# Softmax sums of a transformer block: from pairs of key tiles to running sums over four

## The chip, the cores and the metric

The kernel runs on one core of a Trainium2 chip. The metric is the device time in microseconds (us) of one execution. The engines of the core work side by side, each through its own queue in order: TensorE (PE; its weight loads are shown as PEld), VectorE (DVE), ScalarE (ACT), GpSimd (POOL), and SyncE (SP), which here only issues DMAs. An instruction waits at the head of its queue until what it needs is there, and everything behind it in that queue waits with it.

## What is computed

One pre-norm transformer block in float32 on `x` of 2 x 1024 x 1024, with 32 heads of 32 columns:

```python
qkv = layernorm(x) @ attn_qkvw + attn_qkvb            # 1024 -> 3 x 1024
scores = einsum('bhqd,bhkd->bhqk', q, k) / sqrt(32)
probs = softmax(scores, axis=-1)
x = x + (probs @ v) @ attn_ow + attn_ob
h = layernorm(x)
x = x + (silu(h @ W_gate.T) * (h @ W_up.T)) @ W_down.T  # 1024 -> 2752 -> 1024
```

The softmax needs, for each query, the sum of its 1024 exponentials. The change concerns how this sum is formed.

## The kernel before

**Blocks and units.** Attention is cut into four blocks, here 0 to 3: two batches times two halves of 512 queries (`self.phase` in the code is the block). A block has 16 units, and a unit is two heads by 512 queries. A unit's keys are eight key tiles of 128, so a key tile `p` is a float32 tile of 128 keys by 1024 (two heads by 512 queries). Beside block 0 TensorE runs the projections to Q, K and V; beside blocks 1 to 3 it runs the output projection and the feed-forward of the block before (a seven-product scheme for the matrices, lines 908 to 1090). After block 3 the last feed-forward runs alone.

**What happens to a key tile.** In this order:

1. TensorE makes the scores into PSUM (L509). VectorE takes a running maximum over the tiles (`top`, L525), ScalarE copies the scores to SBUF (`p`, L528).
2. After all eight tiles, VectorE reduces `top` to one negative maximum per query (L548 to L567), which goes through DRAM and comes back on all partitions as `m` (`m<-d`, L575).
3. `less_maximum` adds `m` to the tile: on GpSimd, in block 0 every fourth time on VectorE (L582). ScalarE takes the exponential in place (L591).
4. `add` adds exponentials of neighbouring tiles into each other (L605).
5. `values` has TensorE multiply the tile by the unit's values (`acc<-p,vals`) and, for those tiles in which a sum is complete (`summed`), by a tile of ones (`acc<-p,ones`), both at L620. One such product of a tile is a set of four matmuls that fill four column ranges of the array at once. The ones products give the softmax sums.

**Sums before the change.** In blocks 1 to 3 sums are over two tiles: tile 1 becomes p0+p1, tile 3 becomes p2+p3, and so on. So tiles 1, 3, 5 and 7 get a ones product. Additions for tiles 1 and 5 are GpSimd's, those for 3 and 7 VectorE's. In block 0 sums are over four tiles as a tree, all on VectorE: p1 += p0, p3 += p2, then p3 += p1; so only tiles 3 and 7 get a ones product. As tiles are overwritten with sums, their values have to be replaced by differences, so that the products still add up to the sum of p times v. `differences` (L593) does this on GpSimd once per unit: one operation over 256 columns (L596), and a second one over 128 in block 0 (L599).

**Order.** The kernel sets the order of all instructions itself. `attention_steps` (L650) makes a list of paced steps, called beats, one for each key tile, and the `Emitter` (L44) weaves them into a list of other TensorE work, so that they stand at even distances by planned costs (855 ns for four matmuls' worth). Work of other engines is put off with `em.later(delay, ...)`: it is written down once the planned clock has gone on by so many ns. A tile's subtraction is written at beat n, its exponential 3500 ns later, an addition 8100 ns after the subtraction of the same tile (the third one of block 0: 9900 ns). Value products are written for four tiles together (`RUN`), three beats after the subtraction of the last of the four, once its addition is written. These delays set only the order in the queues; semaphores set the time.

Two things bound this: PSUM has three tiles (`lps`, tag `lin`) for the results of projections and feed-forward, which VectorE and ScalarE read out (for instance L938 to L951 and L1086), and tiles `p` come from a ring of 19 (`RING`).

Of the kernel before, what the change touches and what calls it, by code (L numbers as in the profile page):

```python
# [12 lines left out]
ALU = mybir.AluOpType  # L13
# [117 lines left out]
def preln_block_kernel(  # L131
# [14 lines left out]
    nc = tc.nc  # L146
# [16 lines left out]
    LAG = 3  # L163
    RUN = 4
    RING = NT + LAG + RUN + 4

    const = ctx.enter_context(tc.tile_pool(name="const", bufs=1))
    lin = ctx.enter_context(tc.tile_pool(name="lin", bufs=1))
# [25 lines left out]
    def Pt(name):  # L194
        return att.tile([P, S], F32, tag="p", bufs=RING, name=name)

# [32 lines left out]
    em = Emitter()  # L229
# [234 lines left out]
    class Unit:  # L464
# [114 lines left out]
        def less_maximum(self, kt):  # L579
            p = self.p[kt]  # L580
            eng = nc.vector if self.phase == 0 and kt % 4 == 3 else nc.gpsimd
            eng.tensor_tensor(p, p, self.m, ALU.add)  # L582
            em.later(3500.0, lambda: self.exponential(kt))
            if kt % 2 == 1:
                twice = self.phase == 0 and kt % 4 == 3
                em.later(8100.0, lambda: self.add(kt, 1), None if twice else ("added", self.n, kt))
                if twice:
                    em.later(9900.0, lambda: self.add(kt, 2), ("added", self.n, kt))

        def exponential(self, kt):  # L590
            nc.scalar.activation(self.p[kt], self.p[kt], AF.Exp, scale=SCALE)  # L591

        def differences(self):  # L593

            v = self.v.rearrange("p (i a) n -> p i a n", a=2)
            nc.gpsimd.tensor_tensor(v[:, :, 0, :], v[:, :, 0, :], v[:, :, 1, :], ALU.subtract)  # L596
            if self.phase == 0:
                v = self.v.rearrange("p (i a) n -> p i a n", a=4)
                nc.gpsimd.tensor_tensor(v[:, :, 1, :], v[:, :, 1, :], v[:, :, 3, :], ALU.subtract)  # L599

        def add(self, kt, back):


            eng = nc.vector if self.phase == 0 or kt % RUN == RUN - 1 else nc.gpsimd
            eng.tensor_tensor(self.p[kt], self.p[kt], self.p[kt - back], ALU.add)  # L605

        def summed(self, kt):
            return kt % (4 if self.phase == 0 else 2) == (3 if self.phase == 0 else 1)

        def values(self, kt):  # L610

# [536 lines left out]
    def weight_sum_steps():  # L1148
        q = Steps()

        def start(i):
# [42 lines left out]
            for j, args in enumerate(todo):  # L1194
                em.later(8500.0 + 3000.0 * j, lambda args=args: add(*args))
                em.later(16000.0 + 2500.0 * j, lambda j=j: store(j))
# [158 lines left out]
```

## Time and profile before

| | us |
|---|---|
| median of 3 runs | 3277.49 |
| lowest and highest of them | 3269.68, 3278.75 |
| the profiled execution | 3264.24 |
| its span, first to last instruction | 3262.5 |

Busy time by engine and the stages of the span are in rows shown further below. Some groups of instructions that matter here, with how often they ran, the busy time in all and the mean of one:

| line, engine | what | count | busy us | mean ns |
|---|---|---|---|---|
| L582 POOL | subtract the maximum | 480 | 1193.3 | 2508 |
| L582 DVE | the same, block 0 | 32 | 51.5 | 1610 |
| L591 ACT | exponential | 512 | 533.2 | 1057 |
| L605 POOL | addition of tiles | 96 | 227.1 | 2366 |
| L605 DVE | addition of tiles | 192 | 335.7 | 1748 |
| L620 PE | matmul on values | 4096 | 266.2 | 382 |
| L620 PE | matmul on ones | 1792 | 138.4 | 381 |

How to read it: a float32 matmul stands twice in the records, so 1792 are 896 matmuls. Matmuls overlap each other, so the mean is longer than what one adds to the time. A group's row gives also the idle time of its engine just before its instructions, and what ended it. Idle time of an engine on which nobody waits costs nothing.

### The profile page before, as it was taken

The page shows a single profiled execution, that of the slowest core. Times are in us where ns is not written, and L with a number is a line of the kernel's source. Part 1 is how long each engine was busy: PE and PEld are TensorE (multiplying, and loading weights), DVE is VectorE, ACT ScalarE, POOL GpSimd, SP SyncE. Part 2 cuts the span into 40 slices and gives each one's busy share as a digit, 9 for nine tenths or more (in the row PEclk, how much of TensorE's full clock was granted, in tenths as well). Part 3 has the DMA queues.
Part 4 walks back from the last instruction along what each step waited for, and adds up shares of the span by engine and source line. Part 5 has one row for each costly group of instructions (what it writes and reads, how often), then busy time and mean ns, then how long its engine had stood idle before and what let it go on. Part 6 is the DMA issues. An engine that isn't in the chain of part 4 may idle for free.

```text
span 3262.5 us, 43853 instructions
## 1 busy us (share of the span) xinstructions
PE 3206.8 (98%) x16256; PEld 1792.5 (55%) x16256; DVE 1999.2 (61%) x2733; ACT 1432.7 (44%) x1570; POOL 1767.8 (54%) x871
## 2 busy tenths in 40 slices
PE   8999999999999999999999999999999999999999
PEld 4444444444346565663466555634666567477775
DVE  2266676666356677667766777676677774344334
ACT  2244554444456555554565555545655554010000
POOL 0267766776676555667766665667756555200000
PEclk9999999999999999999999999999999999999999
DMA  4566666655435444446344444463444444544442
GB/s 155 170 183 197 219 197 205 194 173 170 140 107 149 146 147 148 146 149 205 104 142 146 146 143 143 143 201 101 142 147 149 144 139 139 178 156 152 154 153 96
DMA packets 337828, 507.31 MB, mean 155 GB/s; under 512 B 105424, under 2 KB 122064, under 8 KB 337616
## 3 DMA queue, kind: packets, MB, share of 16 engines
q1 hardware_dynamic: 281424, 405.91, 39.9%
q10 hardware_dynamic: 56192, 98.60, 9.8%
q8 instruction: 130, 2.13, 0.3%
q14 instruction: 82, 0.67, 0.1%
HBM read 429.14 MB, written 75.24 MB: 155 GB/s over the span
## 4 chain that ended last, share of the span: by engine, by line
PE 86%; DVE 6%; DMA 3%; POOL 2%; issue 1%; ACT 1%; SPq 0%; ACTq 0%; POOLq 0%; DVEq 0%
PE p L924 31%; PE pq L370 11%; PE pd L1073 11%; PE acc L620 9%; PE s L509 7%; PE pvv L432 7%; PE po L782 7%; DVE top L525 1%; DVE x L1086 1%; POOL p L582 1%; DMA ctx<-dctx 1%; DMA rec<-drec 1%; PE pg L968 1%; PE pd L1000 1%; DVE p L605 1%
## 5 line engine op out<-in xcount | busy, mean ns | idle before, releaser
L582 POOL TENSOR_TENSOR p<-p,m 128x1024 f32<-128x1024 f32 x480 | 1193.3, 2508 | 11.5 <-DVE top L525 8.4
L528 ACT COPY p<-s 128x1024 f32<-128x1024 f32 x512 | 516.7, 1011 | 840.3 <-DVE top L525 642.1
L591 ACT ACTIVATE p<-p 128x1024 f32<-128x1024 f32 x512 | 533.2, 1057 | 270.0 <-POOL p L582 246.2
L525 DVE TENSOR_TENSOR top<-s,top 128x1024 f32<-128x1024 f32 x384 | 468.0, 1219 | 275.1 <-PE s L509 266.1
L924 PE MATMUL p<-sum,m 128*128 128x256 f32 x2688 | 616.7, 383 | 4.1 <-DVE sum L906 3.6
L924 PEld LDWEIGHTS p<-sum,m 128*128 128x128 f32 x2688 | 503.0, 190 | 126.5 <-issue 45.7
L605 POOL TENSOR_TENSOR p<-p,p 128x1024 f32<-128x1024 f32 x96 | 227.1, 2366 | 629.7 <-ACT p L591 595.6
L924 PE MATMUL p<-xn2T,m 128*128 128x256 f32 x2016 | 471.1, 383 | 5.2 <-DVE sum L833 2.4
L370 PE MATMUL pq<-xnT,wqk 128*128 128x512 f32 x1024 | 463.2, 601 | 0.0
L1073 PE MATMUL pd<-wp,h 128*128 128x512 f32 x960 | 438.0, 602 | 10.3 <-DVE x L1086 9.9
L924 PEld LDWEIGHTS p<-xn2T,m 128*128 128x128 f32 x2016 | 376.7, 190 | 104.4 <-issue 47.9
L605 DVE TENSOR_TENSOR p<-p,p 128x1024 f32<-128x1024 f32 x192 | 335.7, 1748 | 135.5 <-ACT p L591 134.8
L370 PEld LDWEIGHTS pq<-xnT,wqk 128*128 128x128 f32 x1024 | 188.2, 190 | 255.9 <-issue 252.7
L1073 PEld LDWEIGHTS pd<-wp,h 128*128 128x128 f32 x960 | 177.1, 190 | 248.1 <-issue 200.0
L509 PE MATMUL s<-q,k 32*128 32x512 f32 x2048 | 302.2, 643 | 10.6 <-ACT p L528 10.5
L1086 DVE TENSOR_TENSOR x<-pd,x 128x512 f32<-128x512 f32 x360 | 236.7, 681 | 71.1 <-PE pd L1073 70.6
L620 PE MATMUL acc<-p,vals 128*32 128x256 f32 x4096 | 266.2, 382 | 5.5 <-DVE p L605 5.4
L1186 POOL TENSOR_TENSOR ws<-raw 128x512 f32<-128x512 f32 x62 | 89.3, 1440 | 300.5 <-DMA raw<-in_w_gu 188.9
L432 PE MATMUL pvv<-wv,xnT 128*128 128x512 f32 x512 | 234.3, 603 | 2.4 <-ACT xnT L266 2.4
L782 PE MATMUL po<-wo,ctx 128*128 128x512 f32 x512 | 234.4, 608 | 0.0
L620 PEld LDWEIGHTS acc<-p,vals 128*32 128x32 f32 x4096 | 119.5, 109 | 147.3 <-issue 71.3
L952 ACT ACTIVATE gate<-gate 128x512 f32<-128x512 f32 x84 | 52.9, 630 | 278.0 <-DVE gate L951 277.4
(94 smaller groups left out, 2476.9 us busy)
## 6 DMA issues: line engine op xcount, KB each, us to landing
m<-dws SPq DMA_DIRECT2D x336, 256.0 KB
m<-in_w_gu SPq DMA_DIRECT2D x252, 256.0 KB
wp<-ddn SPq DMA_DIRECT2D x160, 256.0 KB
m<-d SPq DMA_DIRECT2D x64, 512.0 KB
wp<-in_w_dn SPq DMA_DIRECT2D x120, 256.0 KB
raw<-in_w_gu ACTq DMA_DIRECT2D x84, 256.0 KB
dws<-ws ACTq DMA_DIRECT2D x84, 256.0 KB
x<-in_x SPq DMA_DIRECT2D x32, 512.0 KB
```

Of the source, the lines that this page charges most:

```text
L370: nc.tensor.matmul(ps, wqk[b, g, w, hk][:, k, :], xnT[b, s][:, kc, :], start=(kc == 0), stop=(kc == KC - 1),)
L432: nc.tensor.matmul(st["ps"], xnT[b, t // TB][:, kc, (t % TB) * P : (t % TB + 1) * P], st["w"][kc], start=(kc == 0), stop=(kc == KC - 1),)
L509: nc.tensor.matmul(ps[a][:, h * NH : (h + 1) * NH], self.k[rows, i * P : (i + 1) * P], self.q[rows, :], start=True, stop=True,)
L525: nc.vector.tensor_tensor(self.top, s, self.p[0] if kt == 1 else self.top, ALU.max)
L528: nc.scalar.copy(self.p[kt], s)
L582: eng.tensor_tensor(p, p, self.m, ALU.add)
L591: nc.scalar.activation(self.p[kt], self.p[kt], AF.Exp, scale=SCALE)
L605: eng.tensor_tensor(self.p[kt], self.p[kt], self.p[kt - back], ALU.add)
L620: nc.tensor.matmul(self.acc[j * HD : (j + 1) * HD, c : c + NQ], w(h), self.p[kt][:, q0 : q0 + NQ], start=start, stop=stop, skip_group_chec ...
L782: nc.tensor.matmul(st["ps"], ctxT[b, blk][:, g, t * P : (t + 1) * P], st["w"][hf, g], start=(g == 0), stop=(g == G - 1),)
L924: nc.tensor.matmul(ps, mats[c, n][:, kc, :], rhs, start=(kc == 0), stop=(kc == hk - 1),)
L1073: nc.tensor.matmul(st["pd"], lefts[n](pi)[:, j, t * P : (t + 1) * P], st["wp", pi, n, j], start=(j == 0), stop=(j == PART // 2 - 1),)
```

## The change

All blocks now use sums over four tiles (`SUMS`), formed as a running sum: p1 += p0, p2 += p1, p3 += p2, and the same for tiles 4 to 7. In block 0 all three additions are VectorE's, in blocks 1 to 3 the first two are GpSimd's and the last is VectorE's. Ones products are made for tiles 3 and 7 alone. The delays after the subtraction of the same tile are 8100 ns in block 0, otherwise 9500 ns on GpSimd and 10000 ns on VectorE; an addition whose forerunner isn't written yet is put off by another 500 ns. `differences` becomes three operations over 128 columns each, in all blocks.

```diff
+    SUMS = 4
...
-            if kt % 2 == 1:
-                twice = self.phase == 0 and kt % 4 == 3
-                em.later(8100.0, lambda: self.add(kt, 1), None if twice else ("added", self.n, kt))
-                if twice:
-                    em.later(9900.0, lambda: self.add(kt, 2), ("added", self.n, kt))
+            if kt % SUMS > 0:
+
+                vec = self.phase == 0 or kt % RUN == RUN - 1
+                delay = 8100.0 if self.phase == 0 else 10000.0 if vec else 9500.0
+                eng = nc.vector if vec else nc.gpsimd
+                em.later(delay, lambda: self.add(kt, eng))
...
-            v = self.v.rearrange("p (i a) n -> p i a n", a=2)
-            nc.gpsimd.tensor_tensor(v[:, :, 0, :], v[:, :, 0, :], v[:, :, 1, :], ALU.subtract)
-            if self.phase == 0:
-                v = self.v.rearrange("p (i a) n -> p i a n", a=4)
-                nc.gpsimd.tensor_tensor(v[:, :, 1, :], v[:, :, 1, :], v[:, :, 3, :], ALU.subtract)
-
-        def add(self, kt, back):
-
-
-            eng = nc.vector if self.phase == 0 or kt % RUN == RUN - 1 else nc.gpsimd
-            eng.tensor_tensor(self.p[kt], self.p[kt], self.p[kt - back], ALU.add)
+            v = self.v.rearrange("p (i a) n -> p i a n", a=SUMS)
+            for a in range(SUMS - 1):
+                nc.gpsimd.tensor_tensor(v[:, :, a, :], v[:, :, a, :], v[:, :, a + 1, :], ALU.subtract)
+
+        def add(self, kt, eng):
+
+            if kt % SUMS > 1 and ("added", self.n, kt - 1) not in em.done:
+                em.later(500.0, lambda: self.add(kt, eng))
+                return
+            eng.tensor_tensor(self.p[kt], self.p[kt], self.p[kt - 1], ALU.add)
+            em.done.add(("added", self.n, kt))
 
         def summed(self, kt):
-            return kt % (4 if self.phase == 0 else 2) == (3 if self.phase == 0 else 1)
+            return kt % SUMS == SUMS - 1
```

## The prediction

> **What bounds the kernel now.** I read the totals and the slices first, then busy time by stage, then the waits of TensorE and GpSimd, then the groups that the change touches.
>
> ```profile
> span 3262.5 us, 43853 instructions
> PE 3206.8 (98%) x16256; PEld 1792.5 (55%) x16256; DVE 1999.2 (61%) x2733; ACT 1432.7 (44%) x1570; POOL 1767.8 (54%) x871
> ...
> PE   8999999999999999999999999999999999999999
> ...
> POOL 0267766776676555667766665667756555200000
> PEclk9999999999999999999999999999999999999999
> ```
>
> TensorE has work in 98% of the span, in every slice and at full clock, so a matmul taken away is worth its own length unless a wait takes its place. The stages (start and length, then busy time of PE, PEld, DVE, ACT, POOL):
>
> ```profile
> 160.00:800.00 640.00, 635.97 (x2941) 263.22 (x2940) 428.57 (x446) 309.06 (x338) 460.63 (x244) 1.00 0.61 194
> 800.00:1500.00 700.00, 688.18 (x3888) 395.32 (x3888) 444.44 (x626) 367.93 (x395) 435.54 (x205) 1.00 0.47 142
> 1500.00:2150.00 650.00, 638.26 (x3722) 374.50 (x3723) 459.90 (x636) 354.37 (x378) 424.44 (x196) 0.99 0.49 147
> 2150.00:2790.00 640.00, 626.54 (x3593) 371.69 (x3592) 431.21 (x597) 332.38 (x355) 410.20 (x192) 0.99 0.48 146
> ```
>
> These four rows are attention blocks 0 to 3. TensorE idles 4, 12, 12 and 13 us in them. GpSimd is busy 72% in block 0 and 62 to 65% after it.
>
> **The matmuls that go.** Blocks 1 to 3 hold 48 units. Each unit now runs the ones columns for four of its eight key tiles, afterwards for two: 48 x 2 = 96 sets of four matmuls, 384 in all, and the order of the two builds has exactly these 384 fewer (8256 to 7872). The chain of waits shows what a set takes:
>
> ```profile
> 1550.99 1.07 PE s L509 x8
> 1552.06 3.63 PE po L782 x8
> 1555.69 2.73 PE acc L620 x48
> 1558.42 2.77 PE po L782 x6
> ```
>
> The records count each matmul twice, so x48 is six sets: four on values and two on ones, 2.73 us, or 0.455 us each with the change of tile shape at its ends. The timeline inside such a run has a ones set start 0.43 us before the next set (1518.20 to 1518.63). A run keeps its ends and loses a set from inside, so I take 0.43: 96 x 0.43 = **41 us less on TensorE**. The group row's 138.4 us for 1792 ones records is no price: those records overlap the next set. Block 0 has its four-tile sums already and loses no matmul.
>
> **The additions on GpSimd.** Two more per unit in blocks 1 to 3, 96 in all; the differences of the value tiles become three operations of 128 columns in every unit.
>
> ```profile
> L605 POOL TENSOR_TENSOR p<-p,p 128x1024 f32<-128x1024 f32 x96 | 227.1, 2366 | 629.7 <-ACT p L591 595.6 <-DMA q<-dq 15.5 <-DMA m<-dws 9.7
> ...
> L605 DVE TENSOR_TENSOR p<-p,p 128x1024 f32<-128x1024 f32 x192 | 335.7, 1748 | 135.5 <-ACT p L591 134.8
> ...
> L596 POOL TENSOR_TENSOR vals<-vals 128x256 f32<-128x256 f32 x64 | 56.3, 880 | 0.0
> ...
> L599 POOL TENSOR_TENSOR vals<-vals 128x128 f32<-128x128 f32 x16 | 10.1, 630 | 1.3
> ```
>
> 96 x 2.366 = 227 us, and 48 x (3 x 0.63 - 0.88) = 48 us (block 0: 16 x 0.38 = 6). That is some 92 us a block, and takes GpSimd there from about 64% to about 80%. The cover is the idle time in the first row: 629.7 / 96 = 6.6 us before each GpSimd addition, nearly all spent on the exponential (L591). GpSimd runs ahead and its additions hold it back. Per four tiles the new work is 2.37 + 0.5 = 2.9 us of these 6.6, so I cost it at nothing. With the cover gone, a group would pay up to one addition. In the new order the first addition stands mostly behind the subtraction (L582) of tile 3, no longer of tile 2, and the second behind that of tile 4. So the subtractions run further ahead of their exponentials, and the second addition, due some 5 us before VectorE's, follows an exponential long done. At a unit's end the addition for tile 6 stands behind the next unit's first subtraction, which needs its maximum (DMA `m<-d`). This DMA is issued a median 20 us before the last value matmul, and the subtraction has followed in 4.2 us at the earliest: 4.2 + 2.4 + 2.4 + 1.8 = 11 us. Only some four units (block changes) have less than that; the ends are 0 and 15 us there, and I take 2.
>
> **The last addition moves later on VectorE.** It keeps its count (96 here, 96 in block 0). Its delay after the subtraction grows from 8.1 to 10 us, so it goes behind one or two more PSUM reads. In the order in which the two builds write their instructions, the matmuls between this addition and the first one that reads its tile shrink from 6.8 to 3.8 us in blocks 2 and 3, and from about 7 to about 4.5 in block 1 (at 0.43 us per 256 columns or per set). What that eats is measured in the trace: from the end of the addition to that matmul lie a median 5.2, 3.8 and 3.2 us in blocks 1, 2 and 3. Sliding every addition 2.8 us towards its reader makes TensorE wait 1.5 + 19.4 + 20.5 = 41 us over the 96 groups. That is one end, and by itself it would eat the whole gain. The other end is block 0, which today has a distance of 3.8 us: there TensorE waits 1.1 us for such additions in all 32 groups, though its median slack is 2.5 us. So the ends are 2 and 41 us. Block 0 has no feed-forward work on VectorE, blocks 2 and 3 have, and already wait 4.7 and 7.5 us for it. I therefore stay just above the middle and take 24. Where TensorE waits here VectorE catches up, and some of the 37 us that TensorE idles in these blocks (its waits name ACT `p` L528 and DVE `x` L1086) fall together with the new waits: minus 6.
>
> **Block 0.** The same 96 VectorE additions, but evenly spread (8.1 us after each subtraction) and the last one 1.8 us earlier. VectorE waits 108 us there for exponentials, over two places per group; with three, some 50 us more, in a block where it is idle 211 of 640 us. Gain at most the 4 us that TensorE idles, loss up to 10; I take 0, because the projections' three PSUM tiles cover waits of a few us.
>
> **A rule weighed.** The Trainium skill ("SBUF — State Buffer", the section on who interferes with whom) says that a VectorE instruction with two SBUF inputs and a GpSimd instruction that reads SBUF exclude each other, the later one blocking fully. That speaks against this change: taken whole, 96 GpSimd additions could hold VectorE for 227 us. The rows show the effect and a smaller size. VectorE's addition has a median of 1.23 us and a mean of 1.75, in blocks 1 to 3 of 1.84, so it loses 0.6 us at 64% GpSimd load. At 80% that is 0.15 us more, for about 230 such VectorE operations: 35 us spread over 1990, of which only the last additions (96 x 0.15 = 14 us) stand before a TensorE wait, inside the slack counted above. I take 2, not 227.
>
> **Sum** against the profiled execution (3264.24 us, its span 3262.5): -41 (ones) + 24 (late additions) - 6 (waits that coincide) + 2 (unit ends) + 2 (port) = **-19 us**. The profiled execution lies 13 us under the median of the runs; from the median 3277.5 this gives **3258 us** (-0.6%).
>
> **Rivals.**
> - *The full gain*: the later addition still arrives in time, as in block 0 now. For it: 3.8 us of distance costs block 0 nothing. Against it: VectorE lags further behind in blocks 2 and 3. 3277.5 - 41 = 3236 us.
> - *A wash*: the late additions eat 35 to 50 us, as the uniform slide says. For it: 9 of 32 groups in each of blocks 2 and 3 have under 1.63 us of slack. 3270 to 3285 us, say 3276.
> - *Slower*: VectorE's queue blocks on GpSimd. Its last addition now waits for a GpSimd addition as well as for an exponential, and the PSUM reads of the feed-forward (L938 to L951, L1086) stand behind it, with three PSUM tiles before TensorE stops. If GpSimd's remaining 3.7 us per group don't cover bursts (the bias and context products, L774 and L730, 1.36 us each), each group pays up to one 2.37 us addition; at 0.8 us on average that is 77 us, on top of no other loss, and the time is 3277.5 - 41 + 77 = 3313. It decides from 0.43 us per group on. Against it: the 6.6 us of idle time.
> - *It doesn't do what it says*: the order excludes it; the 384 matmuls are gone.
>
> **Chances.** The forecast case (a gain of 10 to 35 us) 0.42, the full gain 0.15, the wash 0.18, slower 0.25. About 10 us (0.3%) is what a measurement here can tell from no change. So faster 0.57, same 0.18, slower 0.25. The range reaches from the full gain, a little over, to the first half of the slower case: 3234 to 3300. The likeliest case alone spans 3242 to 3268.
>
> **What would show it.** Right: 1024 ones records in place of 1792; value runs of x40, about 0.43 us shorter; GpSimd near 80% in blocks 1 to 3, with shorter waits for L591; TensorE's wait for VectorE's `p` addition up from 12 us to some 30 to 40. Wrong upwards: VectorE's addition waiting on GpSimd's `p`, and TensorE idle growing by over 50 us. Wrong downwards: that TensorE wait staying near 12 us.

## The result

Over 20 runs of each, the changed kernel takes 3280.84 us in the median (3273.92 to 3288.49), the kernel before 3269.38 (3264.63 to 3278.75). The ratio is 1.0032, with a 95% interval of 1.0024 to 1.0040: **slower by about 10 us**, where 19 us faster was forecast. (The median of before is 8 us lower than that of the three runs which the forecast started from.)

The page's totals and slices, of the kernel after:

```profile
span 3272.1 us, 42688 instructions
...
PE 3174.4 (97%) x15488; PEld 1764.7 (54%) x15488; DVE 2046.6 (63%) x2733; ACT 1429.6 (44%) x1570; POOL 2059.1 (63%) x1079
...
PE   8999999999999999998899999989999999999999
...
POOL 0267776786798777677887777778977776200000
PEclk9999999999999999999999999989999999999999
```

TensorE has 32.4 us less to do (3206.8 to 3174.4), and stands idle 42 us more (3262.5 - 3206.8 = 55.7, now 97.7). The difference of the two is the 9.6 us by which the span grew. So the matmuls went, and more than what that saved came back as waiting. The attention blocks say where (busy time of PE, PEld, DVE, ACT, POOL after the length of each stage):

```profile
160.00:800.00 640.00, 632.62 (x2914) 261.85 (x2916) 440.63 (x447) 307.36 (x336) 471.04 (x261) 1.00 0.62 194
800.00:1500.00 700.00, 686.69 (x3692) 391.24 (x3682) 472.94 (x638) 372.13 (x401) 539.46 (x273) 1.00 0.49 145
1500.00:2150.00 650.00, 614.22 (x3396) 358.19 (x3392) 447.09 (x613) 348.48 (x372) 506.29 (x256) 0.98 0.48 143
2150.00:2790.00 640.00, 616.40 (x3366) 363.06 (x3367) 446.28 (x598) 332.61 (x356) 502.83 (x252) 0.98 0.47 143
```

TensorE idles 7 and 13 us in blocks 0 and 1, as before within a few us, but 36 and 24 us in blocks 2 and 3. GpSimd is at 77 to 79%, as forecast. What TensorE waited for, in the whole span (engine and line that waited, the one that released it; total us, times, longest):

```profile
PE acc L622 <- DVE p L606: 35.9, 27, 4.3
PE acc L622 <- POOL p L606: 16.1, 5, 7.1
PE pd L1075 <- DVE x L1088: 11.7, 14, 1.9
```

In the kernel before, TensorE's largest wait in all and the first of the rows above were

```profile
PE s L509 <- ACT p L528: 10.5, 5, 3.9
...
PE acc L620 <- DVE p L605: 5.4, 3, 2.1
```

and none named GpSimd. So value products now wait for sums, 36 us for VectorE's last addition and 16 us for a GpSimd addition, while the wait for ScalarE's copies (`s`) is gone. In blocks 1 to 3 (815 to 2800 us) all TensorE waits other than those at the value products fell from 31.7 to 20.7 us. The new GpSimd additions themselves, and VectorE's, in the page's groups:

```profile
L606 POOL TENSOR_TENSOR p<-p,p 128x1024 f32<-128x1024 f32 x192 | 459.5, 2393 | 359.7 <-ACT p L593 350.6
...
L606 DVE TENSOR_TENSOR p<-p,p 128x1024 f32<-128x1024 f32 x192 | 362.0, 1885 | 122.8 <-ACT p L593 94.5
```

GpSimd still has 360 us of idle time before its additions. It isn't short of time in all, yet too late at some places. The longest such place is at the change from block 1 to 2 (timeline of GpSimd, VectorE and TensorE, start and duration, idle time before and its releaser in brackets, rows of other work between them left out):

```profile
1498.12 1.27 POOL L732 TENSOR_TENSOR ctx<-ctx,rec 128x512 f32<-128x512 f32 x1 [2.17 <-DMA rec<-drec]
...
1506.71 1.51 POOL L599 TENSOR_TENSOR vals<-vals 128x128 f32<-128x128 f32 x3
...
1508.18 2.34 POOL L583 TENSOR_TENSOR p<-p,m 128x1024 f32<-128x1024 f32 x1
1510.47 2.35 POOL L606 TENSOR_TENSOR p<-p,p 128x1024 f32<-128x1024 f32 x1
...
1512.79 7.95 POOL L583 TENSOR_TENSOR p<-p,m 128x1024 f32<-128x1024 f32 x3
...
1512.85 3.36 DVE L606 TENSOR_TENSOR p<-p,p 128x1024 f32<-128x1024 f32 x1 [8.32 <-POOL p L606]
...
1512.87 1.08 PE L622 MATMUL acc<-p,vals 128*32 128x256 f32 x8 [7.15 <-POOL p L606]
...
1516.27 1.08 PE L622 MATMUL acc<-p,vals 128*32 128x256 f32 x8 [2.31 <-DVE p L606]
```

The addition for tile 6 stands behind the differences and the next unit's first subtraction, and further ahead GpSimd had waited for a DMA before the context products (L732). VectorE idles 8.3 us at its own addition, TensorE 7.2 us, and then TensorE waits 2.3 us more for VectorE. VectorE's addition takes 3.36 us there, where its median in blocks 1 to 3 of the kernel before is 1.22: GpSimd's next subtraction starts 0.06 us ahead of it, and 3.36 is near the length of a subtraction (2.34) and of a short addition together. It is a chain of two queues blocked at their heads. What it doesn't show is whether such waits at the value products are the cause or only the place where the loss comes out.

### The profile page after: what moved, and what is told of

It is laid out like the page before. It is cut to its first block, busy times and chain, and to the rows that moved or that the text cites. A ratio compares the mean times of both kernels' runs of the same rounds, so it can differ in the third digit from the quotient of the medians.

```text
span 3272.1 us, 42688 instructions
## 1 busy us (share of the span) xinstructions
PE 3174.4 (97%) x15488; PEld 1764.7 (54%) x15488; DVE 2046.6 (63%) x2733; ACT 1429.6 (44%) x1570; POOL 2059.1 (63%) x1079
## 5 line engine op out<-in xcount | busy, mean ns | idle before, releaser
L583 POOL TENSOR_TENSOR p<-p,m 128x1024 f32<-128x1024 f32 x480 | 1220.8, 2561 | 12.5 <-DMA m<-d 11.4
L606 POOL TENSOR_TENSOR p<-p,p 128x1024 f32<-128x1024 f32 x192 | 459.5, 2393 | 359.7 <-ACT p L593 350.6
L606 DVE TENSOR_TENSOR p<-p,p 128x1024 f32<-128x1024 f32 x192 | 362.0, 1885 | 122.8 <-ACT p L593 94.5
L622 PE MATMUL acc<-p,vals 128*32 128x256 f32 x4096 | 259.2, 387 | 52.4 <-DVE p L606 35.9
L510 PE MATMUL s<-q,k 32*128 32x512 f32 x2048 | 294.8, 640 | 0.0
L1088 DVE TENSOR_TENSOR x<-pd,x 128x512 f32<-128x512 f32 x360 | 236.9, 681 | 56.6 <-PE pd L1075 55.6
```

What stands on the lines that cost most here:

```text
L510: nc.tensor.matmul(ps[a][:, h * NH : (h + 1) * NH], self.k[rows, i * P : (i + 1) * P], self.q[rows, :], start=True, stop=True,)
L606: eng.tensor_tensor(self.p[kt], self.p[kt], self.p[kt - 1], ALU.add)
L622: nc.tensor.matmul(self.acc[j * HD : (j + 1) * HD, c : c + NQ], w(h), self.p[kt][:, q0 : q0 + NQ], start=start, stop=stop, skip_group_chec ...
L1088: nc.vector.tensor_tensor(xs, st["pd"], xs, op)
```

## The experiments

All times are against runs of the kernel before on the same chip; kernels of different groups are compared by their ratios to it. The runs have numbers, which the texts use: 1 to 3 shift the delays, 4 leaves out the matmuls, 5 loads GpSimd, 6 to 10 read the sums later, 11 and 12 put more on VectorE, 13 and 15 to 17 move both ends (there is no 14). The letters for theories in the expectations: Q, VectorE's last addition stands too late in its queue; G, GpSimd gives its tile too late, at block changes above all; P, GpSimd's load by itself, through the port that it shares with VectorE; L, lateness of the sums alone; A, GpSimd and VectorE stand in each other's way at the heads of their queues.

### What the removed matmuls are worth

The kernel before, with the ones products of tiles 1 and 5 left out in blocks 1 to 3:

```diff
-            if self.summed(kt):
+            if self.summed(kt) and kt % 4 == 3:
```

> The kernel before without the ones products of tiles 1 and 5 in blocks 1 to 3, so 384 matmuls fewer and nothing else (the sums then lack those pairs). This prices the matmuls that the change removes: at 0.43 us a set 41 us less than the kernel before. If they were hidden behind other engines, under 15 us.

Measured: 3233.71 us against 3272.84, ratio 0.9884 (0.9865 to 0.9904), so **38 us less**. The price of 0.43 us a set holds. The changed kernel gives back all of that and 10 us more, some 49 us in all.

### The delays of the change

```diff
-                delay = 8100.0 if self.phase == 0 else 10000.0 if vec else 9500.0
+                delay = 8100.0 if vec else 9500.0      # e1: VectorE earlier
+                delay = 8100.0 if self.phase == 0 else 10000.0 if vec else 8100.0  # e2: GpSimd earlier
+                delay = 8100.0                         # e3: both
```

> The changed kernel with one number back: VectorE's last addition is written 8.1 us after the subtraction in all blocks (10 before), GpSimd's stay at 9.5. Theory Q (the loss is VectorE's additions standing too late in their queue, each wait of TensorE made dearer by a lower granted clock after it): TensorE's waits on VectorE's addition fall from 90 us (both rows) to under 40, and the time falls by 20 to 35 us, to about 20 under the kernel before. Rival G (GpSimd gives the tile too late, at block changes above all): the wait only moves from VectorE's queue position to GpSimd's addition, and the time stays within 8 us of the changed kernel's. Rival P (GpSimd's larger load slows VectorE through the shared port): no change.

> The changed kernel with GpSimd's additions written 8.1 us after the subtraction (9.5 before), VectorE's at 10 as in the change. This puts the addition for tile 6 ahead of the next unit's first subtraction, which needs that unit's maximum. Rival G: the waits of TensorE at tiles 2 and 6 (16 us, on GpSimd's addition) and those that follow at tiles 3 and 7 go, and with them some 10 us of low clock: 20 us or more faster than the changed kernel. Theory Q: at most 16 us faster, and the waits on VectorE's addition in quiet stretches stay. Rival P: no change.

> The changed kernel with all additions written 8.1 us after their subtractions. If Q and G both hold, their gains add up: 35 to 50 us faster than the changed kernel, 25 to 40 us faster than the kernel before. Rival P: within 8 us of the changed kernel.

Measured: 3282.10 (ratio 1.0037, 1.0021 to 1.0053), 3271.28 (1.0003, 0.9990 to 1.0015) and 3270.61 us (1.0003, 0.9992 to 1.0015), with the kernel before at 3272.84. Q alone falls: with VectorE earlier nothing is gained. G is right in part: GpSimd's additions one place earlier bring about 10 us, half of what G named. Those 10 us also lie within the 16 that Q allowed for that run. Both together bring no more than one. The waits of the first of these show why (rows on the additions, here and in what follows from 815 to 2800 us, blocks 1 to 3, where nothing else is said):

```profile
DVE p L606 <- POOL p L606: 68.7, 13, 15.3
...
PE acc L622 <- DVE p L606: 21.0, 13, 3.9
...
PE acc L622 <- POOL p L606: 19.0, 5, 5.5
```

TensorE's wait for VectorE's addition fell from 35 to 21 us (in the measure of the expectation, which adds the waits of matmuls and of weight loads, from 90 to 54, not under 40). But VectorE now sat 69 us at the head of its queue (28 in the changed kernel) because GpSimd wasn't done.

### GpSimd's load without its waits

To the fourth kernel are added two GpSimd operations per unit, on tiles of the same size, that nobody waits for (1.98 us each, where a GpSimd addition takes 2.38). The run also has eight weight tiles in place of nine, to make room for the spare tile:

```diff
+            if self.phase > 0 and kt % 4 == 2:
+                em.later(9500.0, lambda: nc.gpsimd.tensor_tensor(spare, spare, spare, ALU.mult))
```

> The fourth experiment (the kernel before without the 384 ones matmuls) plus 2 independent GpSimd multiplications of 128x1024 per unit in blocks 1 to 3, 96 in all, on a spare tile that nobody else touches: the GpSimd load of the change without any of its waits. Nine weight tiles become eight to make room. Rival P (GpSimd's load costs through the shared port): 15 us or more over the fourth experiment (so at most 24 us under the kernel before), with VectorE's mean addition above 2.0 us. Theory L (what costs is only that sums come too late for their readers): within 6 us of the fourth experiment, 33 to 40 us under the kernel before.

Measured: 3253.65 against 3271.26 us, ratio 0.9948 (0.9932 to 0.9964): 18 us under the kernel before, about **20 us over the kernel without them** (by the two intervals, 13 to 29). That is within P's expectation. The groups of VectorE in blocks 1 to 3, of the kernel before and of this one:

```profile
L605 DVE TENSOR_TENSOR p<-p,p 128x1024 f32<-128x1024 f32 x95 | 174.4, 1836 | 30.1 <-ACT p L591 29.8
```

```profile
L609 DVE TENSOR_TENSOR p<-p,p 128x1024 f32<-128x1024 f32 x96 | 220.1, 2293 | 34.5 <-ACT p L595 34.4
```

The fourth kernel's mean is 1821 ns, so more work on GpSimd makes the same addition 0.47 us longer, 45 us in all. TensorE's wait for it at the value products was 11.1 us in the fourth kernel and is 26.7 here; it is the one wait of TensorE that grew much. So the load's cost reaches the time at least in part by making the last addition late. Not all of it need be the port: the multiplications also stand in GpSimd's queue. ScalarE's exponentials waited 194 us for subtractions here and 142 in the fourth kernel, and VectorE's additions 34 us for exponentials, 20 in the fourth. The run doesn't separate the two ways. (The profile is that of the slowest of its six executions, 3260.90 us.)

### Reading the sums later

If lateness is all, a value product that comes one beat later must cure it. Three kernels did that with `n - NT - LAG - 4` in place of `- 3`, a ring of 20 tiles and eight weight tiles in place of nine:

> The second experiment (GpSimd's additions at 8.1 us, VectorE's at 10) with the value products one beat (some 5 us) later, a ring of 20 tiles and eight weight tiles in place of nine. Theory L: TensorE's waits at the value products fall under 15 us (42 in the second experiment), the low clock after them goes, and the time is 25 to 38 us under the kernel before. Rival P: still within 12 us of the kernel before, as VectorE and GpSimd hold each other up wherever the reader stands.

> The changed kernel itself with its own delays (9.5 and 10), the value products one beat later, the ring and the weight tiles as in the run before this. Theory L: 5 us more distance covers VectorE's late additions and most of GpSimd's at block changes (7 us at the most), so 20 to 35 us under the kernel before. Rival P: within 12 us of it.

> Control: the fourth experiment (no ones products of tiles 1 and 5 in blocks 1 to 3) with the value products one beat later, ring 20 and eight weight tiles. All theories: within 6 us of the fourth experiment, so 33 to 45 us under the kernel before. If it is more than that apart, the later reading or the weight tiles cost or bring something by themselves.

Measured: 3282.86, 3309.72 and 3242.22 us, with the kernel before at 3271.26. All three missed, and can't be read as meant: the last value products of a unit now came after the loading of the values of the unit after next into the same buffer, used these values, and waited for the load. With the loading a beat later too:

```diff
-                if kt == NT - 2:
+                if kt == NT - 1:
                     q.add(units[k].load_v, needs=("v", units[k].b, units[k].hf))
```

> The sixth run again (GpSimd's additions at 8.1, VectorE's at 10, value products one beat later, ring of 20, eight weight tiles), with the loading of the next but one unit's values also one beat later, so that it no longer overtakes the value products that still read the old ones. If only lateness costs (theory L): 25 to 38 us under the kernel before. If GpSimd's load costs by itself what the fifth run showed (21 us, theory P) and lateness the rest: 10 to 20 us under the kernel before. If the later reading makes waits elsewhere: not under it.

> Control of the run before this: the kernel before without the 384 ones matmuls, value products and the loading of values one beat later, ring of 20, eight weight tiles. 33 to 42 us under the kernel before, as the fourth experiment; the eighth run's lack of 9 us was the overtaken loading (TensorE waited 9 us for it). If it stays near 29 us under, the later reading costs by itself.

Measured: 3267.61 (ratio 0.9988, 0.9980 to 0.9996) and 3230.95 us (0.9875, 0.9858 to 0.9891), with the kernel before at 3271.03. The control shows that reading later costs nothing. But the ninth run is only 3 us under the kernel before, below what L and P named, although no matmul of a value product waits for a sum in it any more. **Lateness at the reader alone falls as the cause.** What is waited for, in blocks 1 to 3:

```profile
ACT p L593 <- POOL p L583: 336.2, 119, 13.2
...
DVE p L606 <- POOL p L606: 23.9, 7, 5.0
...
PE pd L1075 <- DVE x L1088: 22.6, 25, 3.2
...
PE s L510 <- ACT p L529: 16.5, 7, 4.8
...
PE pd L1002 <- DVE x L1013: 8.6, 2, 4.8
```

ScalarE waits 336 us for subtractions, twice the 170 us of the control. The suspicion was that GpSimd's additions, at 8.1 us, stand ahead of subtractions and hold them up while they wait for their own exponentials. ScalarE and VectorE also read PSUM, and TensorE now waits for these reads (`s`, `pd`). This run alone doesn't show that ScalarE's wait is what costs the time; the fifteenth below bears on it.

### Both ends apart

So GpSimd's additions go back to 9.5, and VectorE's last one from 10 to 13, with the later reading. (The ninth run lies 37 us over its control, 3267.61 against 3230.95, and not 27 as the first expectation has it.)

```diff
-                delay = 8100.0 if self.phase == 0 else 10000.0 if vec else 9500.0
+                delay = 8100.0 if self.phase == 0 else 13000.0 if vec else 9500.0
```

> As the ninth run (value products and value loads one beat later), but GpSimd's additions back at the change's 9.5, so that a subtraction stands ahead of each addition, and VectorE's last addition at 13. In the ninth run TensorE no longer waited at the value products, and yet lost 27 us more than its control, while ScalarE's exponentials waited 336 us for GpSimd's subtractions (170 in the control). Theory A (GpSimd's additions stand in the way of the next subtractions, ScalarE waits for these and reads PSUM later): ScalarE's wait falls under 200 us, VectorE's on GpSimd under 10, and the time to 18 to 35 us under the kernel before. Rival P (port load alone, 20 us): 12 to 20 under it. Rival C (the later reading or clock dips eat it): within 8 us of it.

> The run before this with VectorE's last addition at 10 as in the change, so the changed kernel's own delays with value products and value loads one beat later. Against the run before it shows what VectorE loses by reaching its addition before GpSimd is done. Theory A: VectorE waits 30 us or more for GpSimd at its head and PSUM reads behind it are late: 8 us or more slower than the run before this. Otherwise equal within 4 us.

> As the thirteenth kernel (9.5 and 13, later reading), but the addition for tile 6 at 8.1, ahead of the next unit's first subtraction and its wait for the maximum. Theory A says that the exponentials then wait a little more: within 6 us of the thirteenth. If unit ends are what is left: 6 us or more faster.

> The changed kernel with VectorE's last addition at 13 (10 before) and nothing else, so the reader stays where it was: the fourth corner beside the changed kernel (10, old reader), the fifteenth (10, later reader) and the thirteenth kernel (13, later reader; 52 us faster than the fifteenth). Theory A with both ends (VectorE's addition must stand far enough behind GpSimd's and far enough ahead of the reader, and one beat is too short for both): the waits at the value products rise above 60 us and the time is 15 us or more over the changed kernel's. If VectorE's blocked queue alone is the loss: 20 us or more faster than the changed kernel.

| VectorE's addition at | reader as in the change | reader one beat later |
|---|---|---|
| 10 us | 1.0032 (the change) | 1.0045 (1.0032 to 1.0059) |
| 13 us | 1.0234 (1.0209 to 1.0260) | **0.9883** (0.9870 to 0.9897) |

The four corners, GpSimd's additions at 9.5 in all of them. Neither step alone brings anything: the later reader alone leaves the loss, the later addition alone makes it 76 us instead of 10. Together they give 3232.67 us against 3271.93, **38 us under the kernel before**, which is all that the missing matmuls are worth. The sixteenth (tile 6 early) gave 3243.60 us, ratio 0.9917 (0.9903 to 0.9930): 11 us slower than that, where theory A allowed 6. ScalarE's wait for subtractions rises to 237 us there, and TensorE's for VectorE's additions from 7 to 14.

Theory A is right only in part. In the thirteenth run ScalarE's wait fell to 191 us, as it said; VectorE's wait for GpSimd did not fall under 10 us (26.5), and the gain is larger than the range. What A said of the fifteenth and the seventeenth run, waits and times, held. The step of GpSimd's additions from 8.1 to 9.5 alone, the ninth against the fifteenth run, brought ScalarE's wait back to 174 us and yet made the time longer (0.9988 to 1.0045), with VectorE's wait for GpSimd up from 24 to 46 us. So ScalarE's wait does not set the time by itself. The corner with GpSimd at 8.1, VectorE at 13 and the later reader wasn't run; whether 9.5 is needed stays open.

The two kernels with the later reader differ only in the place of VectorE's 96 additions, and by 52 us. Waits in blocks 1 to 3 with the addition at 10:

```profile
ACT p L593 <- POOL p L583: 174.2, 56, 11.5
...
DVE p L606 <- POOL p L606: 46.4, 9, 8.1
...
PE pd L1075 <- DVE x L1088: 28.0, 29, 3.5
...
PE pd L1002 <- DVE x L1013: 21.0, 2, 10.5
...
PE acc L622 <- DVE p L606: 2.7, 1, 2.7
```

and at 13:

```profile
DVE p L606 <- POOL p L606: 26.5, 7, 7.3
...
PE pd L1075 <- DVE x L1088: 15.4, 19, 1.9
...
PE acc L622 <- DVE p L606: 7.1, 3, 5.1
...
PE pd L1002 <- DVE x L1013: 0.9, 1, 0.9
```

The waits at the value products (`acc`) are small in both. What differs most is `pd`, PSUM results of the feed-forward that VectorE reads too late: the two rows make 33 of the 44 us that TensorE idles more (120.4 against 75.9 us in the whole span). VectorE's queue and TensorE's at the second block change show one of the two waits of 10.5 us, with the addition at 10:

```profile
1508.50 0.68 DVE L1033 TENSOR_TENSOR x<-x,x 128x512 f32<-128x512 f32 x1
1516.41 3.34 DVE L606 TENSOR_TENSOR p<-p,p 128x1024 f32<-128x1024 f32 x1 [7.23 <-POOL p L606]
1519.67 1.87 DVE L1013 TENSOR_TENSOR x<-pd,x 128x512 f32<-128x512 f32 x3
```

```profile
1507.64 2.31 PE L1002 MATMUL pd<-wd,h 128*128 128x512 f32 x5
1520.41 4.57 PE L1002 MATMUL pd<-wd,h 128*128 128x512 f32 x6 [10.46 <-DVE x L1013]
```

VectorE stands 7.2 us before an addition whose GpSimd part isn't there, then takes 3.3 us for it, and three finished PSUM tiles wait behind. TensorE runs out of PSUM. At the other wait of 10.5 us, at 2189 us, it is the same: 7.6 us before the addition, three reads behind it. With the addition at 13 VectorE waits as long at that block change, but two PSUM reads stand behind the addition and not three:

```profile
1507.57 3.35 DVE L606 TENSOR_TENSOR p<-p,p 128x1024 f32<-128x1024 f32 x1 [7.27 <-POOL p L606]
1510.84 1.27 DVE L1013 TENSOR_TENSOR x<-pd,x 128x512 f32<-128x512 f32 x2
```

TensorE isn't held by them; it idles 4.7 us, for a copy by ScalarE, in place of 10.5. And with 13 and the old reader TensorE simply waits for the sum: 103.6 us on VectorE's additions over the whole span, 58 times.

### More of it on VectorE

Two kernels try to spare GpSimd: block 0's tree in all blocks, with one GpSimd addition per four tiles as before, and the running sum on VectorE alone.

```diff
-                twice = self.phase == 0 and kt % 4 == 3
+                twice = kt % 4 == 3                    # e11, on the kernel before
...
-                vec = self.phase == 0 or kt % RUN == RUN - 1
+                vec = True                             # e12, on the changed kernel, delay 8100
```

> The kernel before with block 0's tree over four tiles in all blocks: GpSimd keeps the one addition per four tiles that it had in blocks 1 to 3, VectorE makes two (96 more in all, some 1.8 us each, 175 us in the 1990 us of these blocks). The same 384 matmuls go. If GpSimd's load and its place in the chain are what spoils the change: 15 to 35 us under the kernel before. If any addition after the old ones comes too late or VectorE is full: within 10 us of it or slower.

> The changed kernel with all three additions of four tiles on VectorE in all blocks (8.1 us after the subtraction), as in its block 0: GpSimd has 192 additions fewer than in the change and 96 fewer than before, VectorE 192 more than either (some 1.4 us each, 270 us in blocks 1 to 3, from 67% to 80% busy). Less contention at the port, but a full VectorE queue: if the port and GpSimd's place are all that matters, 20 to 40 us under the kernel before; if VectorE's queue is the bound, 10 us or more over it.

Measured: 3301.11 (ratio 1.0097, 1.0079 to 1.0115) and 3350.03 us (1.0224, 1.0203 to 1.0244), with the kernel before at 3271.03. Both are slower, with VectorE busy 65 and 69% of the span and GpSimd less than in the changed kernel. In the tree TensorE waits 62.7 us for VectorE's additions at the value products, in the running sum 49 us for PSUM reads of `pd`. Both kept the old distance to the reader, so they show that sparing GpSimd doesn't save the change, and leave open what they would do with a later reader.

## Why the prediction was wrong

The sum counted 41 us less TensorE work and 22 us more TensorE waiting (24 - 6 + 2 + 2). The profiles show 32.4 us less work and 42 us more waiting. The step that failed is the price of the longer chain: GpSimd's additions were "costed at nothing" from an average idle time, and VectorE's last addition was taken as late for one reader only, not as an instruction that also waits for GpSimd at the head of VectorE's queue. In its place the runs show a chain whose links hold each other up: with the same instructions, the later reader and VectorE's addition at 13 in place of 10, the loss is gone (1.0045 to 0.9883). In detail:

- **The matmuls**: 41 us expected, 38 measured by themselves. Right.
- **GpSimd "costed at nothing"**: of the 6.6 us of idle time per group 3.7 are left (359.7 us over 96 groups), just as the prediction's 6.6 - 2.9 has it, but an average doesn't help at a block change. "Only some four units (block changes) have less than that" and "I take 2" became 16 us of TensorE's time on GpSimd's additions, in five waits. The wait looked at was that for the maximum alone; the additions also stand behind the differences and, at block changes, behind the context products (L732), which wait for a DMA.
- **The last addition**: 24 us, measured 30 us more on TensorE's wait for it (5.4 to 35.9). That is near in size partly by luck, and wrong in kind. (The 4.7 and 7.5 us that blocks 2 and 3 "already wait" count the same waits for matmuls and again for weight loads: TensorE's matmuls waited 5.4 us in all. In the prediction's measure its sign, 12 us to some 30 to 40, went to 90.) The prediction saw one end, the distance to the reader, which was a cost to be made smaller by writing the addition earlier. The first and third runs did so and gained nothing beyond GpSimd's part. The other end is GpSimd's second addition. The old distance to the reader was enough for a chain of one addition after the exponential, and isn't for one of two or three over two engines.
- **"Where TensorE waits here VectorE catches up: minus 6"**: TensorE's other waits in blocks 1 to 3 did fall, by 11 us. The wait for ScalarE's copies (L528, 10.5 us) is gone, that of `pd` for `x` stayed (L1086: 9.9 us before; L1088: 11.7 after). That they fell because they coincide with the new waits isn't shown.
- **The port: "I take 2"**: the load alone cost about 20 us in the fifth run, with VectorE's additions 0.47 us longer where 0.15 was estimated. The 14 us were counted as lying "inside the slack counted above", which the late additions had already used. It isn't a fixed price of the load: the thirteenth kernel carries the same GpSimd additions and has the whole gain, and its VectorE additions take a mean of only 1694 ns in blocks 1 to 3 (1836 before, 2027 in the changed kernel, 2068 in the fifteenth). Why they are shorter there isn't shown.
- **Block 0**: 0 expected. TensorE's idle time there went from 4 to 7 us.
- **The rival that came true** is the slower one by its mechanism (VectorE's queue blocked by GpSimd, PSUM reads behind it), together with the forecast's own late addition. By size it is between the wash (3276) and it (3313): 42 us of additional waiting over 96 groups are 0.44 us a group, where the rival took 0.8 and named 0.43 as the point from which it decides. Its price per group was an average; in truth much of the loss sits in few places: between 1480 and 1600 and between 2130 and 2270 us, around two block changes, TensorE's gaps sum to 36.7 us (12.9 before), out of 72.7 in blocks 1 to 3 (37.7 before).
- **The signs**: 1024 ones records, GpSimd at 77 to 79% and shorter waits for L591 (596 to 351 us) came as named. So did the first sign of "wrong upwards": VectorE's addition waits 28 us for GpSimd, where it waited for none before. TensorE's idle time grew by 42 us, a little under the 50 of the second.

Adding up the profiled runs: -32.4 us of TensorE work, +31 us for VectorE's additions, +16 for GpSimd's, -5 for the rest, which makes +9.6. Why 41 us of matmuls make only 32.4 of busy time stays open; the last section has what the traces say of it.

## What to carry to other kernels

When a change makes a chain between two engines longer by a link, look for the reader's distance from the chain's start, not for the engines' idle time: each link wants its place in an in-order queue, late enough not to block that queue and early enough for the next. If one step of a move gains nothing and another alone loses, try them together before giving the move up; here the two corners of +0.45% and +2.3% lie beside one of -1.2%. And what stands behind a waiting instruction matters more than the wait: VectorE waited 7 us at the same block change with its addition at 10 and at 13. At 10 three PSUM reads stood behind it and TensorE idled 10.5 us; at 13 two stood there, and it idled 4.7 us.

## What was not expected of the hardware

A wait of TensorE is followed by a stretch at a lower clock. The stretches around the 7.15 us wait shown above, in the changed kernel (length, busy times of PE, PEld, DVE, ACT and POOL, then the granted clock, the share of DMA and GB/s):

```profile
1505.00:1513.00 8.00, 0.85 (x20) 0.28 (x16) 0.15 (x1) 3.51 (x4) 7.84 (x7) 0.82 0.69 245
1513.00:1520.00 7.00, 4.69 (x26) 1.51 (x26) 4.41 (x3) 3.02 (x4) 7.00 (x3) 0.50 0.16 37
1520.00:1530.00 10.00, 10.00 (x41) 3.66 (x43) 7.66 (x11) 4.94 (x5) 10.00 (x6) 0.98 0.50 181
```

For 7 us after the wait the granted clock is 0.50, and TensorE waits 2.3 us more in them. The Trainium skill ("TensorE: Matmul & The Clock Gate", Part 1) says that the clock falls to half after one idle window of about 3.4 us and comes back after as long a busy one; the sum forecast no such term. In this trace a wait of 2.25 us at 1531.2 was followed by a low clock as well (0.62 from 1533.5 to 1538), so the window of the page isn't a safe limit here. How much of the loss it is remains open. An upper estimate from the mean clocks: 0.4% of 3262 us were held back before and 0.9% of 3272 after, so 16 us more at most, less what fell into idle time. TensorE's busy time is 12 us more in the changed kernel (3174.4) than in the fourth (3162.5), which runs the same matmuls; but it is 19 us more than in the thirteenth (3155.4) too, and that has the whole gain at a lower mean clock (0.989, against 0.991 in the changed kernel, 0.994 in the fourth and 0.996 before).
